# GpSimd's row scalings at fixed places, row tails in two parts, and one transpose for the softmax denominators of all eight heads

## The chip, the core and the metric

The kernel runs on one core of one Trainium2 chip. The metric is device time in microseconds (us) of one execution, less is better. Five engines matter: TensorE (PE in the profile, with its weight loads as PEld) multiplies matrices into PSUM, VectorE (DVE) and ScalarE (ACT) read PSUM and work element by element, GpSimd (POOL) works element by element on SBUF and issues transfers, and SyncE (SP) issues transfers. Each engine carries out its instructions in the order in which the program lists them; an instruction that waits holds back all that stand behind it on that engine.

## What is computed

One layer of a graph transformer with masked attention, two layer norms and a feed-forward part, and one more residual layer norm around the whole. F = 8 frames, N = 2048 rows, C = 256 channels, H = 8 heads of D = 32, all in float32:

```python
qkv = jnp.einsum('fnc,ck->fnk', x, w_qkv)                 # x: (8, 2048, 256)
q, k, v = jnp.split(qkv, 3, axis=-1)                      # each to (F, N, 8, 32)
scores = jnp.einsum('fnhd,fmhd->fhnm', q, k) / jnp.sqrt(D)
scores = jnp.where(adj > 0, scores, -1e9)                 # adj: (2048, 2048)
attn = softmax(scores, axis=-1)
t = jnp.einsum('fhnm,fmhd->fnhd', attn, v).reshape(F, N, C)
y = layernorm(x + t, ln1_g, ln1_b)
h = relu(einsum('fnc,cd->fnd', y, w1) + b1)
y = layernorm(y + einsum('fnd,dc->fnc', h, w2) + b2, ln2_g, ln2_b)
return layernorm(x + y)                                   # no gain, no offset
```

## The kernel before, in words

**Items.** The queries of a frame are cut into four chunks of 512 (`qc`), the heads into two groups of four (`g`), the keys into sixteen blocks of 128 (`mb`). An item is `(f, qc, g, mb)`; there are 8 x 4 x 2 x 16 = 1024, worked in that order. For one item TensorE makes the scores of 128 keys against 512 queries for four heads (`scores`, L230), VectorE adds the mask out of PSUM in two halves (L233), ScalarE takes the exponential in place (L237), and TensorE multiplies by V and accumulates over the 16 blocks (`values`, L249). The exponentials are never divided block by block; the sums over the keys (the denominators) are made apart.

**Denominators.** A group of 16 items leaves 16 tiles of exponentials in the pool `p` of 12 buffers. `add_up` adds most of them into three tiles: GpSimd adds blocks 3, 6, 8, 10, 12 and 14 into block 0 (L271), and transfers that accumulate, issued from GpSimd's queue (L268), add blocks 4, 7 and 11 into block 1 and 5, 9 and 13 into block 2. `denominator` then multiplies the three and block 15 by a matrix of ones (L315, 16 float32 matmuls in four blocks, each head's sum over 32 identical rows), ScalarE copies the result to `dT` (L317), TensorE turns `dT` in four transposes (L95, in `transposes`), and VectorE takes the reciprocal (L326) and notes the sum and the smallest sum (L327, L328). This is done for each half of the heads.

**Row tails.** When the second group of a chunk is done, `outcome` turns and divides the attention output (`divide`, L353), adds x by an accumulating transfer (L339), and starts `tail`: `norm`, `feed_forward` (two turns, two products by w1, the scaling of the rows by gain and offset on GpSimd at L459 and L461, two products by w2 whose results VectorE adds at L483), `norm`, a second scaling on GpSimd (L363, L365), x added by another accumulating transfer (L367), seven steps of waiting, `norm`, and the store (L370). A `norm` is four pairs of statistics on VectorE (L278, L279), four small GpSimd instructions (L283 to L287), and, two steps later, four scalings on ScalarE (L290). `y` has two buffers, so at most two tails are under way: a third `outcome` waits at `ROOM` until one has stored. The last chunk of all is finished by `finish`, in two half-tiles that take turns.

**Order of work.** The order on every engine is written out by the program, one step per item. Step t first calls `advance(t)`, which lets side work on; then it issues the exponential of item t + 1, the scores of item t + 2, and the values of item t. Side work is a list of generators, sorted by due step. `BANK` asks for the one PSUM bank of side work; one generator may take it in a step, and holds it while it answers `MORE` or `WAIT`. A holder that answers `MORE` goes on in the same step if at least 1024 of a credit are left (2200 come in with each step, and 512 columns in four heads cost 2048, a set of turns 1400) or if something that wants the bank is past its due step; otherwise it goes on in the next step. I call what fits one step at the usual rate a portion: one block of denominators, half of a projection, half of a w1 or w2 product pair, or one set of four turns. A number given to `yield` makes a generator sleep that many steps. Tails start ten steps after their `outcome` is due and are due 16 steps later still (the last but one: five and three). The work for the next frame (`turn`, `ask`, `project`) starts at the steps in `NEXT`; projected keys and values have 11 buffers each, of which a frame uses eight.

**After the items.** `while fill: advance(t, finish=True)` runs what is left, without credit. `finish` lists all steps of both halves in one go.

## Time and profile before

| what | value |
|---|---|
| median of 3 runs | 3196.82 us (3194.78 to 3200.07) |
| the profiled execution's own time | 3199.32 us |
| its span, first to last instruction | 3197.5 us |
| mean granted TensorE clock | 0.987 |
| busy: PE, DVE, POOL, ACT | 3098.8, 2737.4, 2589.4, 2438.4 us |
| turns of `dT`: 256 matmul instructions | 48.1 us busy |
| waits of TensorE for VectorE's mask additions, whole span | 35.6 us in 61 waits |
| the same between 200 and 3000 us | 11.0 us in 26 waits |

The profiled execution took 2.5 us more than the median, and 1.8 us of its time lie outside the span. Busy times are unions of an engine's instructions. Idle time of an engine that does not bound the kernel costs nothing, so the table has to be read with the question of which engine the others wait for. In a timeline row the first number is the start, the second the length over which merged instructions extend, and a bracket gives the idle time before and what ended it.

### The profile page before, as it was taken

To read this page: it belongs to the slowest core of one execution; us is meant where nothing else is said; L and a number is where in the kernel's file an instruction comes from. 1 tells how busy PE (TensorE), PEld (TensorE's weight loads), DVE (VectorE), ACT (ScalarE), POOL (GpSimd) and SP (SyncE) were. 2 spreads that over 40 slices of the span, in tenths; PEclk is the share of its full clock that TensorE was granted. 3 is DMA by queue.
4 is the path that set the end of the run, shared out by engine and by line. 5 is a ranking of instruction groups with operands and counts; after the bars stand their busy time and mean duration, and the time that the engine had idled before them with its cause. 6 is when DMAs were issued, how large, how long until landed. Compare 5 with 4: busy or idle time off the path is not lost.

```text
span 3197.5 us, 68542 instructions
## 1 busy us (share of the span) xinstructions
PE 3098.8 (97%) x28996; PEld 980.3 (31%) x28996; DVE 2737.4 (86%) x3203; ACT 2438.4 (76%) x1941; POOL 2589.4 (81%) x1358
## 2 busy tenths in 40 slices
PE   7899999999999999999999999999999999999985
PEld 4222333233332333323333323323233233332222
DVE  4788888888889988888988988888888888889975
ACT  3677778778778777788777788778878778778764
POOL 0478888888888888789888889888888788879884
PEclk8899999999999999999999999999999999999998
DMA  9588889788879888789878889878889788878863
GB/s 322 141 193 189 181 180 194 178 190 193 182 175 210 186 191 175 175 193 208 190 172 176 190 185 221 174 169 199 180 193 207 170 191 196 178 170 167 178 142 71
DMA packets 153098, 589.49 MB, mean 184 GB/s; under 512 B 15024, under 2 KB 67760, under 8 KB 103888
## 3 DMA queue, kind: packets, MB, share of 16 engines
q0 software_dynamic: 64272, 433.75, 67.7%
q1 hardware_dynamic: 87696, 149.98, 13.4%
q8 instruction: 229, 3.75, 0.4%
q10 hardware_dynamic: 816, 1.31, 0.1%
q14 instruction: 85, 0.70, 0.1%
HBM read 146.67 MB, written 37.75 MB: 58 GB/s over the span
## 4 chain that ended last, share of the span: by engine, by line
PE 87%; DVE 5%; issue 2%; DMA 1%; POOL 1%; ACT 1%; DVEq 0%; ACTq 0%; POOLq 0%
PE s L230 32%; PE x L249 28%; PE x L54 16%; PE x L315 7%; DVE p L233 4%; PE x L95 4%; DMA p<-p 1%; DVE st L278 0%; POOL p L271 0%; DMA y<-in_x_dram 0%; DVE y L353 0%; ACT p L237 0%; PE s L54 0%; DVE mv L279 0%; ACT y L290 0%
## 5 line engine op out<-in xcount | busy, mean ns | idle before, releaser
L233 DVE TENSOR_TENSOR p<-s,mask 128x1024 f32<-128x1024 f32 x2048 | 2410.3, 1219 | 336.2 <-PE s L230 196.0
L237 ACT ACTIVATE p<-p 128x2048 f32<-128x2048 f32 x1024 | 1956.6, 1911 | 527.7 <-DVE p L233 453.7
L271 POOL TENSOR_TENSOR p<-p 128x2048 f32<-128x2048 f32 x382 | 1858.7, 4866 | 388.5 <-ACT p L237 388.2
L230 PE MATMUL s<-qT,kT 32*128 32x512 f32 x8192 | 1172.4, 642 | 40.9 <-DVE p L233 35.6
L249 PE MATMUL x<-p,v 128*32 128x512 f32 x8192 | 1092.7, 605 | 0.5 <-ACT oT L253 0.4
L230 PEld LDWEIGHTS s<-qT,kT 32*128 32x128 f32 x8192 | 320.8, 183 | 643.9 <-DVE p L233 602.5
L268 POOL DMA_DIRECT2D p<-p x382 | 408.1, 1070 | 78.4 <-ACT p L237 49.4
L249 PEld LDWEIGHTS x<-p,v 128*32 128x32 f32 x8192 | 161.4, 108 | 779.9 <-issue 289.8
L315 PE MATMUL x<-p,ones 128*32 128x512 f32 x2080 | 267.1, 592 | 0.6 <-DMA p<-p 0.5
L54 PE MATMUL x<-in,wqkv 128*32 128x512 f32 x1888 | 243.5, 592 | 0.0
L290 ACT ACTIVATE y<-y,nb,rs 128x256 f32<-128x256 f32 x372 | 218.4, 590 | 3.0 <-POOL nb L287 3.0
L278 DVE BATCH_NORM_STATS2 st<-y 128x6 f32<-128x256 f32 x372 | 155.1, 417 | 5.2 <-DMA y<-in_x_dram 5.2
L54 PE MATMUL x<-turned,w1s 128*32 128x512 f32 x992 | 122.5, 592 | 0.0
L54 PEld LDWEIGHTS x<-wqkv,in 128*32 128x32 f32 x3584 | 102.2, 110 | 63.5 <-issue 58.9
L54 PE MATMUL x<-w2s,hT 128*32 128x256 f32 x2016 | 121.1, 381 | 0.0
L54 PE MATMUL x<-wqkv,in 128*32 128x128 f32 x3584 | 117.3, 273 | 0.0
L315 PEld LDWEIGHTS x<-p,ones 128*32 128x32 f32 x2080 | 67.4, 110 | 156.8 <-issue 152.0
L54 PEld LDWEIGHTS x<-in,wqkv 128*32 128x32 f32 x1888 | 61.7, 110 | 140.9 <-issue 113.1
L284 POOL TENSOR_TENSOR rs<-rs,mhalf 128x4 f32<-128x4 f32 x93 | 96.2, 1035 | 7.7
L363 POOL TENSOR_TENSOR y<-y,g2r 128x1024 f32<-128x1024 f32 x31 | 99.3, 3205 | 1.9 <-ACT y L290 1.9
L365 POOL TENSOR_TENSOR y<-y,be2r 128x1024 f32<-128x1024 f32 x31 | 91.9, 2963 | 0.6
L54 PEld LDWEIGHTS x<-w2s,hT 128*32 128x32 f32 x2016 | 65.5, 111 | 70.5 <-issue 37.8
(116 smaller groups left out, 1342.1 us busy)
## 6 DMA issues: line engine op xcount, KB each, us to landing
p<-p POOLq DMA_DIRECT2D x382, 1024.0 KB, 9.7
in<-xd SPq DMA_DIRECT2D x87, 512.0 KB, 9.3
mask<-md SPq DMA_DIRECT2D x248, 128.0 KB, 7.9
y<-in_x_dram POOLq DMA_DIRECT2D x62, 512.0 KB, 9.5
p<-in_adj_dram SPq DMA_DIRECT2D x16, 1024.0 KB, 9.7
out_dram<-y SPq DMA_DIRECT2D x31, 512.0 KB, 5.9
in<-in_x_dram SPq DMA_DIRECT2D x29, 512.0 KB, 14.5
xd<-in SPq DMA_DIRECT2D x28, 512.0 KB, 10.7
```

The costliest lines, as they stand in the source:

```text
L54: nc.tensor.matmul(out[r:r + D], lhsT[:, r:r + D], rhs, start=start, stop=stop)
L95: nc.tensor.transpose(ps[:, j * P:(j + 1) * P], s, ident)
L230: nc.tensor.matmul(ps2[half][:, j, :], KT[f, mb // TPC, g][r:r + D, (mb % TPC) * P:(mb % TPC + 1) * P], QT[f, qc, g][r:r + D, :], start=Tr ...
L233: nc.vector.tensor_tensor(pt[:, 2 * half:2 * half + 2, :], ps, MK[f, qc, mb // 2][:, mb % 2, None, :].to_broadcast([P, 2, CH]), ALU.add)
L237: nc.scalar.activation(PT[item], PT[item], AF.Exp, scale=1.0 / math.sqrt(D))
L249: nc.tensor.matmul(O[grp][r:r + D, :], V[f, mb // TPC, g][:, mb % TPC, r:r + D], PT[item][:, h, :], start=(mb == 0), stop=(mb == LAST))
L268: nc.gpsimd.dma_start(PT[f, qc, g, chain[0]], PT.pop(item), accum_op=ALU.add)
L271: nc.gpsimd.tensor_tensor(first, first, PT.pop(item), ALU.add)
L278: nc.vector.bn_stats(st, t[:, j, :])
L290: nc.scalar.activation(t[:, j, :], t[:, j, :], AF.Identity, bias=nb[:, j:j + 1], scale=rs[:, j:j + 1])
L315: nc.tensor.matmul(ps[r:r + D, :], cst["ones"], term[:, h, :], start=(n == 0), stop=(n == len(blocks) - 1))
L363: nc.gpsimd.tensor_tensor(z, z, rows(cst["g2r"]), ALU.mult)
```

## The change

It has four parts, in the words of the code.

1. **Denominators.** The ones are replaced by a matrix `halves` that has, for group g, ones in 16 of the 32 columns and zeros in the others. The sums of the two groups so land in different rows of a tile. For g = 0 ScalarE copies the PSUM tile to `dT` and the generator ends; for g = 1 VectorE adds the PSUM tile to it, `dT` is turned once for both, and one reciprocal and one pair of notes cover all eight heads. The fourth block of a group may come one step later.
2. **GpSimd's scalings.** Both instructions of a scaling are issued together, at a step chosen by `calm`: at once if the next block number is among 15, 0, 1, 2, 3, 4, otherwise not before block 15 comes. The first scaling runs in a generator of its own beside the w1 products, and the w2 products wait until four steps after it. `norm` leaves 2, 3 or 4 steps before its ScalarE part, by a table (`lag`).
3. **Tails in two parts.** What comes after the w1 products is a generator of its own (`closing`) with its own due step, 33 steps after the outcome's; the first part is due at 27. The last tail but one starts at 8 in place of 5, loads x into a tile and adds that on GpSimd (its offset `be2r` is not added in this branch) in place of the offset, the accumulating transfer and seven steps, and takes its last `norm` in one go. `finish` takes its tile from the pool `p` and sleeps a step between rounds from the fourth on.
4. **Buffers and places.** Keys and values have 10 buffers in place of 11, and five of the eight projections of a frame start later.

```diff
...
     dp = ctx.enter_context(tc.tile_pool(name="dp", bufs=1, space=bass.MemoryType.DRAM))
     mkp = ctx.enter_context(tc.tile_pool(name="mkp", bufs=MB // 2 + 1))
     ld = ctx.enter_context(tc.tile_pool(name="ld", bufs=LD))
-    kp = ctx.enter_context(tc.tile_pool(name="kp", bufs=3 * NCK - 1))
+    kp = ctx.enter_context(tc.tile_pool(name="kp", bufs=3 * NCK - 2))
     qp = ctx.enter_context(tc.tile_pool(name="qp", bufs=4))
-    vp = ctx.enter_context(tc.tile_pool(name="vp", bufs=3 * NCK - 1))
+    vp = ctx.enter_context(tc.tile_pool(name="vp", bufs=3 * NCK - 2))
     pp = ctx.enter_context(tc.tile_pool(name="pp", bufs=12))
     work = ctx.enter_context(tc.tile_pool(name="work", bufs=1))
     yp = ctx.enter_context(tc.tile_pool(name="yp", bufs=2))
...
         give(xT)
 
 
-    PT, O, OT, RC = {}, {}, {}, {}
+    PT, O, OT, RC, DT = {}, {}, {}, {}, {}
 
     def scores(item):
         f, qc, g, mb = item
...
             first = PT[f, qc, g, POOLED[0]]
             nc.gpsimd.tensor_tensor(first, first, PT.pop(item), ALU.add)
 
+
+    CALM = (LAST, 0, 1, 2, 3, 4)
+
+    def calm():
+        return 1 + (LAST - 1 - state["now"]) % MB if (state["now"] + 1) % MB not in CALM else 1
+
+    def lag():
+        return (4, 4, 4, 4, 2, 2, 2, 2, 2, 2, 3, 3, 3, 4, 4, 4)[state["now"] % MB]
 
     def norm(t, per=1):
         mv = small.tile([P, TPC, nc.vector.BN_AGGR_DIM], F32, name="mv")
...
         nb = small.tile([P, TPC], F32, name="nb")
         nc.gpsimd.tensor_tensor(nb, mv[:, :, 0], rs, ALU.mult)
         nc.gpsimd.tensor_scalar(nb, nb, -1.0, 1.0, op0=ALU.mult, op1=ALU.mult)
-        yield 2
+        yield lag()
         for j in range(TPC):
             nc.scalar.activation(t[:, j, :], t[:, j, :], AF.Identity, bias=nb[:, j:j + 1], scale=rs[:, j:j + 1])
             if j % per == per - 1:
...
     def denominator(f, qc, g, ready):
         grp = (f, qc, g)
         blocks = [ALONE, MOVED[0][0], POOLED[0], MOVED[1][0]]
-        late = {2: ready - 1, 3: ready}
+        late = {2: ready - 1, 3: ready + 1}
         if (f, qc, g) == items[-1][:3]:
             blocks = [POOLED[0], 11, 12, MOVED[0][0], 13, 14, MOVED[1][0], 15]
             late = {n: len(items) - k for n, k in ((2, 2), (3, 1), (4, 1), (5, 0), (6, 0), (7, 0))}
...
             state["credit"] -= 4 * CH
             for h in range(4):
                 r = D * h
-                nc.tensor.matmul(ps[r:r + D, :], cst["ones"], term[:, h, :], start=(n == 0), stop=(n == len(blocks) - 1))
-        dT = op.tile([P, CH], F32, name="dT")
-        nc.scalar.copy(dT, ps)
+                nc.tensor.matmul(ps[r:r + D, :], cst["halves"][:, g, :], term[:, h, :], start=(n == 0), stop=(n == len(blocks) - 1))
+        if g == 0:
+            DT[f, qc] = op.tile([P, CH], F32, name="dT")
+            nc.scalar.copy(DT[f, qc], ps)
+            return
+        dT = DT.pop((f, qc))
+        nc.vector.tensor_tensor(dT, ps, dT, ALU.add)
         yield 1
         yield BANK
         ps = bank()
         transposes(ps, [dT[:, j::TPC] for j in range(TPC)])
-        if g == 0:
-            RC[f, qc] = op.tile([P, TPC, H], F32, name="rc")
-        rc = RC[f, qc]
-        den = ps.rearrange("p (j c) -> p j c", c=P)[:, :, ::D]
-        nc.vector.reciprocal(rc[:, :, 4 * g:4 * g + 4], den)
+        rc = RC[f, qc] = op.tile([P, TPC, H], F32, name="rc")
+        den = ps.rearrange("p (j c) -> p j c", c=P)[:, :, ::D // 2]
+        nc.vector.reciprocal(rc, den)
         nc.vector.tensor_tensor(RS[:, 0], RS[:, 0], den, ALU.add)
         nc.vector.tensor_tensor(RS[:, 1], RS[:, 1], den, ALU.min)
-        if g == 1:
-            begin = items.index((f, qc, g, LAST)) + SUM + 2
-            start(begin, outcome(f, qc) if (f, qc) != (F - 1, NCK - 1) else finish(f, qc), begin)
+        begin = items.index((f, qc, g, LAST)) + SUM + 2
+        start(begin, outcome(f, qc) if (f, qc) != (F - 1, NCK - 1) else finish(f, qc), begin)
 
     def outcome(f, qc):
         yield ROOM
...
         nc.gpsimd.dma_start(y, xin, accum_op=ALU.add)
         begin = items.index((f, qc, 1, LAST)) + SUM + 2
         if (f, qc) == (F - 1, NCK - 2):
-            start(begin + 5, tail(f, qc, y, xin, 2), begin + 8)
+            xb = take([P, TPC, C], F32)
+            nc.sync.dma_start(xb, xin)
+            start(begin + 8, tail(f, qc, y, xin, begin + 11, 2, xb), begin + 11)
         else:
-            start(begin + 10, tail(f, qc, y, xin), begin + 26)
+            start(begin + 10, tail(f, qc, y, xin, begin + 33), begin + 27)
 
     def divide(f, qc, y):
         rc = RC.pop((f, qc))
...
             transposes(ps, [oT[:, j::TPC] for j in range(TPC)])
             nc.vector.tensor_tensor(y[:, :, gg * P:(gg + 1) * P].rearrange("p j (h d) -> p j h d", d=D),
                                     ps.rearrange("p (j h d) -> p j h d", h=4, d=D),
-                                    rc[:, :, 4 * gg:4 * gg + 4, None].to_broadcast([P, TPC, 4, D]), ALU.mult)
-
-    def tail(f, qc, y, xin, per=1):
+                                    rc[:, :, gg::2, None].to_broadcast([P, TPC, 4, D]), ALU.mult)
+
+    def tail(f, qc, y, xin, due, per=1, xb=None):
         yield from norm(y, per)
-        yield from feed_forward(y)
+        second = yield from feed_forward(y, xb is not None)
+        start(state["now"] + 1, closing(f, qc, y, second, xin, per, xb), due)
+
+    def closing(f, qc, y, second, xin, per, xb):
+        yield from second
         yield 1
         z = y
         yield from norm(z, per)
-        nc.gpsimd.tensor_tensor(z, z, rows(cst["g2r"]), ALU.mult)
-        yield 1
-        nc.gpsimd.tensor_tensor(z, z, rows(cst["be2r"]), ALU.add)
-        yield 1
-        nc.gpsimd.dma_start(z, xin, accum_op=ALU.add)
-        yield 7
-        yield from norm(z, per)
+        if xb is None:
+            yield calm()
+            nc.gpsimd.tensor_tensor(z, z, rows(cst["g2r"]), ALU.mult)
+            nc.gpsimd.tensor_tensor(z, z, rows(cst["be2r"]), ALU.add)
+            yield 1
+            nc.gpsimd.dma_start(z, xin, accum_op=ALU.add)
+            yield 7
+        else:
+            nc.gpsimd.tensor_tensor(z, z, rows(cst["g2r"]), ALU.mult)
+            nc.gpsimd.tensor_tensor(z, z, xb, ALU.add)
+            yield 2
+        yield from norm(z, per if xb is None else TPC)
         nc.sync.dma_start(out[f, qc * CH:(qc + 1) * CH, :].rearrange("(p j) c -> p j c", p=P), z)
         state["tails"] -= 1
 
...
         nc.sync.dma_start(dst[:, own], z)
 
     def finish(f, qc):
-        y = yp.tile([P, TPC, C], F32, name="y")
+        y = pp.tile([P, 4, CH], F32, name="p")[:, 0:2, :].rearrange("p a (b c) -> p (a b) c", c=C)
         xr, xb = state["rows"]
         yield from divide(f, qc, y)
         yT, hT = (work.tile([P, 2, CH], F32, name=n) for n in ("turned", "hT"))
         dst = out[f, qc * CH:(qc + 1) * CH, :].rearrange("(p j) c -> p j c", p=P)
         both = [half_rows(h, y, xr, xb, yT, hT, dst) for h in range(2)]
+        rounds = 0
         while both:
             for e in list(both):
                 if next(e, both) is both:
                     both.remove(e)
-
-    def feed_forward(y):
+            rounds += 1
+            if rounds > 3:
+                yield 1
+
+    def feed_forward(y, soon):
         yield TURNED
         state["turned"] = True
         yT = work.tile([P, 2, CH], F32, name="turned")
...
             ps = bank()
             transposes(ps, [y[:, j, a * P:(a + 1) * P] for j in range(TPC)])
             nc.scalar.activation(yT[:, a, :], ps, AF.Identity, bias=cst["be1c"][:, a:a + 1], scale=cst["g1c"][:, a:a + 1])
-        yield 1
-        nc.gpsimd.tensor_tensor(y, y, rows(cst["g1r"]), ALU.mult)
-        yield 1
-        nc.gpsimd.tensor_tensor(y, y, rows(cst["be1b2r"]), ALU.add)
+        scaled = []
+
+        def scale():
+            nc.gpsimd.tensor_tensor(y, y, rows(cst["g1r"]), ALU.mult)
+            nc.gpsimd.tensor_tensor(y, y, rows(cst["be1b2r"]), ALU.add)
+            scaled.append(state["now"])
+
+        def later():
+            yield calm()
+            scale()
+
+        if soon:
+            scale()
+        else:
+            start(state["now"], later(), state["now"])
         hT = work.tile([P, 2, CH], F32, name="hT")
         for d in range(2):
             yield BANK
...
                 columns(ps, w1s[:, a, d * P:(d + 1) * P], yT[:, a, :], start=(a == 0), stop=(a == 1))
             nc.scalar.activation(hT[:, d, :], ps, AF.Relu, bias=cst["b1s"][:, d:d + 1], scale=1.0)
         state["turned"] = False
-        yield 1
+        return second_products(y, hT, scaled)
+
+    def second_products(y, hT, scaled):
+        while not scaled or state["now"] < scaled[0] + 4:
+            yield 1
         z = y
         for jj in range(0, TPC, 2):
             yield BANK
...
         give(xT)
 
     NEXT = {1: [(turn, 0)], 2: [(ask, 1)], 20: [(turn, 1)], 34: [(ask, 2)], 40: [(project, 0, 0)], 50: [(turn, 2)],
-            60: [(project, 1, 0)], 66: [(ask, 3)], 72: [(turn, 3)], 80: [(project, 2, 0)], 98: [(ask, 0)], 100: [(project, 3, 0)],
-            104: [(project, 0, 1)], 108: [(project, 1, 1)], 112: [(project, 2, 1)], 116: [(project, 3, 1)]}
+            60: [(project, 1, 0)], 66: [(ask, 3)], 72: [(turn, 3)], 98: [(ask, 0)], 100: [(project, 2, 0)],
+            104: [(project, 3, 0)], 108: [(project, 0, 1)], 112: [(project, 1, 1)], 116: [(project, 2, 1)], 120: [(project, 3, 1)]}
 
     def begin():
         todo = deque((qc, c) for qc in range(NCK) for c in range(NCK))
...
     nc.gpsimd.memset(cst["ones"], 1.0)
     cst["mhalf"] = const.tile([P, TPC], F32, name="mhalf")
     nc.gpsimd.memset(cst["mhalf"], -0.5)
-    RS = const.tile([P, 2, TPC, H // 2], F32, name="RS")
+    cst["halves"] = const.tile([P, 2, D], F32, name="halves")
+    nc.gpsimd.memset(cst["halves"], 0.0)
+    for g in range(2):
+        nc.gpsimd.memset(cst["halves"][:, g, g * D // 2:(g + 1) * D // 2], 1.0)
+    RS = const.tile([P, 2, TPC, H], F32, name="RS")
     nc.gpsimd.memset(RS[:, 0], 0.0)
     nc.gpsimd.memset(RS[:, 1], 1.0)
```

## The prediction

> **What bounds the kernel now.** I read three views first: the page's head, the windows, and the waits between 200 and 3000 us.
>
> ```profile
> PE 3098.8 (97%) x28996; PEld 980.3 (31%) x28996; DVE 2737.4 (86%) x3203; ACT 2438.4 (76%) x1941; POOL 2589.4 (81%) x1358
> ```
>
> ```profile
> 1500.00:2000.00 500.00, 498.59 (x4692) 156.18 (x4692) 438.46 (x506) 395.72 (x316) 426.86 (x220) 1.00 0.85 190
> 3000.00:3100.00 100.00, 88.56 (x708) 24.50 (x708) 86.44 (x106) 73.73 (x57) 88.23 (x50) 0.95 0.79 165
> ```
>
> ```profile
> PE s L230 <- DVE p L233: 11.0, 26, 0.7
> ```
>
> The window's columns are length, busy PE, PEld, DVE, ACT and POOL, then granted clock. From about 100 to 2900 us TensorE is busy without a break, at full clock, and waits 11.0 us in all; the others have 12% or more to spare. GpSimd, which half of the diff is about, is waited for almost nowhere: the addition at L271 kept TensorE's loads waiting 1.3 us in the whole run. So the middle is bought with TensorE time alone, and VectorE (86%) is next.
>
> How much an instruction of TensorE is worth is seen in its timeline, cut at the first score matmul of each item (L230):
>
> ```profile
> 3058.06 1.04 PE L315 MATMUL x<-p,ones 128*32 128x512 f32 x8
> 3059.03 1.14 PE L230 MATMUL s<-qT,kT 32*128 32x512 f32 x8
> ...
> 3061.95 1.14 PE L230 MATMUL s<-qT,kT 32*128 32x512 f32 x8
> 3063.02 1.06 PE L249 MATMUL x<-p,v 128*32 128x512 f32 x8
> 3064.02 0.75 PE L95 MATMUL x<-ident,dT 128*128 128x128 f32 x4
> 3064.70 1.14 PE L230 MATMUL s<-qT,kT 32*128 32x512 f32 x8
> ...
> 3094.00 1.14 PE L230 MATMUL s<-qT,kT 32*128 32x512 f32 x8 [0.42 <-DVE p L233]
> 3095.07 1.07 PE L249 MATMUL x<-p,v 128*32 128x512 f32 x8
> 3096.55 1.14 PE L230 MATMUL s<-qT,kT 32*128 32x512 f32 x8 [0.41 <-DVE p L233]
> ```
>
> The step with one block of denominators lasts 2.92 us (3059.03 to 3061.95), the one that turns `dT` 2.75, an empty one 2.55, because two mask additions keep VectorE 2 x 1.22 us. I cut all steps of items 33 to 895 so (863 steps, 2572.3 us): 109 hold two portions (3.78 to 3.81 us), 16 are empty, the rest hold one. One more portion in a step costs 0.86 us, so scores and values alone cost TensorE 2.92 - 0.86 = 2.06.
>
> At the end two things stand out, in the timelines of VectorE, TensorE and the stores:
>
> ```profile
> 3081.76 0.43 DVE L278 BATCH_NORM_STATS2 st<-y 128x6 f32<-128x256 f32 x1 [5.23 <-DMA y<-in_x_dram]
> 3084.20 2.09 PE L230 MATMUL s<-qT,kT 32*128 32x512 f32 x8 [6.61 <-DVE p L233]
> ```
>
> ```profile
> 3184.66 3.94 SPq L435 DMA_DIRECT2D out_dram<-y  x2
> 3193.33 0.33 SPq L370 DMA_DIRECT2D out_dram<-y  x1
> ```
>
> The last tail but one starts its statistics before x has been added to its rows; VectorE stands 5.23 us, and TensorE behind it. And the store that ends the kernel is not that of the last chunk (second of L435, about 3188.3) but that of this same tail, whose last statistics the program lists behind all of `finish`.
>
> **The change, part by part.** The sum is against the profiled execution, 3199.3 us.
>
> *Denominators.* Of 64 sets of four turns 32 go. A set takes TensorE 0.68 us (3064.02 to 3064.70). Frames 0 to 6 have 28 chunks: 28 x 0.68 = 19.0 us, if the step is filled with other work or a double step becomes a single one; if the step stays empty it gets shorter by 2.75 - 2.55 = 0.20 only. I take 19.0, because the list of side work is longer than the steps: a chunk has 36 portions for 32 steps (35 after), which is why 109 steps were double. The 16 matmuls of a group keep their shapes. ScalarE loses 32 copies of 0.585 us (L317), 18.7; it is not waited for, worth nothing. VectorE gains 32 additions as at L483, 0.69 each, 22 us, and loses 32 sets of L326 to L328 (240 + 111 + 158 ns, 16 us); 6 us more in 2737, hidden by its 12% in the middle. Behind the addition stand the next mask additions: at 3061.98 the denominators ended and the copy began at 3062.09, a mask addition at about 3062.6, so 0.69 us of addition holds it back 0.2 us, less than the 0.3 us that VectorE idles in such a step. The side bank comes free 0.1 us later than by the copy; its next user starts 2 us later. The fourth block's extra step changes nothing: at one block a step, from step 2, it never came before step 5.
>
> *Empty steps.* Each costs 2.55 - 2.06 = 0.49 us of TensorE. The w2 products were past due in every middle chunk (52 banks, each both portions in one step); with the later due step about half should spread. Moving projections from step 80 to 100 and on thins out the third quarter of a frame (27 portions for its 32 steps). Bounds: all 16 vanish, -7.8 us; two more per frame, +7. The two moves oppose each other; I take 0.
>
> *GpSimd's scalings, `lag`.* Nearly the same instructions at other steps; the nearest rows of what they could free are waits of 1.3 us (TensorE's loads for L271) and 3.0 us (ScalarE L290 for L287). I take 0. What they make longer is the tail, see the second rival. The buffers and the three GpSimd fills at the start (0.17 us each, as L812, after the identity is made) cost nothing: TensorE waits there for x and the identity.
>
> *Last frame.* It has 27 empty steps of 127, for lack of the next frame's work. Four sets of turns at 0.20 are 0.8; a few double steps that spread into empty ones (0.49 each) another 1.2: -2, bounds -0.8 and -4.7.
>
> *The stall at 3076.* The tail starts three steps later, some 3 x 2.45 us for VectorE, more than the 5.23 it stood. But its `outcome` waits for the first tail of the frame, which is longer now: counted in steps below it stores one step later than `outcome` ran before, and then x's transfer stands behind one more addition of 4.9 us on GpSimd's queue. So 7.4 - 4.9 = 2.5 us of the 5.23 go. TensorE lost 6.61 for 5.23; I take -3. Bounds -6.3 (step of 8.75 us to an empty one of 2.49) and 0.
>
> *The end.* If the last norm of this tail is listed ahead, the end is the store at 3188.3: -5.0. Against it: its second norm now reaches ScalarE only behind the last exponentials and `oT` (3151.6). 2.1 us of scalings (L290 x4) and two GpSimd instructions of 2.4 end at about 3158.6. Its four statistics stand on VectorE between the two divisions of `finish`, which went at 3155.6 and 3156.2, and take 2.1 us: the second division moves to 3160.8, +4.6. I take 0, bounds -5.0 and +4.6.
>
> Sum: -19.0 - 2 - 3 = -24.0, that is 3175.3. The profiled execution took 2.5 more than the median: 3173.
>
> *A rule that speaks against it.* TensorE's steps got longer by 0.86 us per portion in the rows above. The Trainium skill, "Perfetto Trace Analysis", Identifying the Most-Contended Engine, says that matmul busy time is no good measure of TensorE's headroom and to judge by the weight loads' share, here 31%. By that TensorE has room and the 19.0 would be 0: 3192. The rows decide for me, since 109 double steps show what a portion costs.
>
> **Rivals.**
>
> *All of it counts.* Empty steps vanish, the stall goes whole, the end is the earlier store: 19.0 + 7.8 + 4.7 + 6.3 + 5.0 = 42.8, so 3154. For it: later due steps spread the doubles. Against it: the longer tail and the thinner third quarter.
>
> *The tail gets too long (slower).* From the step in which `outcome` is due: statistics at 10 to 13, ScalarE at 18, turns at 22, first scaling at 26, the next group's denominators hold the bank from 28 to 31, w2 at 32 to 34, second norm from 35, ScalarE at 42, second scaling at 47, transfer at 48, third norm from 55, ScalarE at 63, store at 67. Before, it was 58. The third `outcome` is due at 64 and so waits three steps, and its own tail starts at 74 whether x has come or not. In the trace the latest of these transfers was issued at 1361.23, landed 9.3 us later (the median) and was used at 1374.43, 3.9 us to spare. One step later it stands behind an addition of 5.1 us and comes 1.2 us late, 3.6 with the longest landing (11.7). VectorE then stands, in all 28 chunks, with all mask additions behind it: at 2 us, 56 us, 3173 + 56 = 3229. It decides from 24/28 = 0.86 us per chunk. A second norm that begins one step later than 35 misses its place, and `calm` sends the scaling ten steps on: worse. Against it: step 67 leaves the transfer where it was in the latest case.
>
> *Freed steps stay empty.* VectorE becomes the bound in them: 32 x 0.20 + 3 = 9.4, so 3187. For it: 2.55 against 2.75 in the rows; against it: 36 portions for 32 steps.
>
> *It does not do what it says:* the turns are covered by VectorE anyway, the end is eaten by the additions: 3197.
>
> **How the numbers follow.** Likeliest, 3163 to 3183: 0.58. All of it, below: 0.14. Empty steps, 3183 to 3194: 0.16, a quarter of it within 0.2%, which is about what can be told here (6.4 us: 3190.4 to 3203.2). Tail too long: 0.10, four fifths of it slower. Nothing: 0.02. Faster 0.58 + 0.14 + 0.12 = 0.84; same 0.04 + 0.02 + 0.02 = 0.08; slower 0.08. The range runs from the rival of all gains, 3153, into that of empty steps, 3191.
>
> **What would show it.** 128 turns of `dT` in place of 256, about 24 us busy; PE busy near 3077; additions of 0.69 us at the new line; fewer w2 steps with both portions. The 5.23 us wait halved. The middle step count: if empty steps rise over 30, the third rival. If VectorE's statistics wait for `y<-in_x_dram` in the middle, the second. I am wrong if the tails' order makes VectorE or GpSimd late in every chunk, which this trace cannot show.

## The result: 8.4% slower, and the profile after

| | before | changed |
|---|---|---|
| median | 3197.40 us (3194.78 to 3200.07, 4 runs) | 3464.62 us (3457.25 to 3471.02, 4 runs) |
| ratio | | 1.0835, 95% interval 1.0811 to 1.0859 |
| span of the profiled execution | 3197.5 us | 3460.7 us |
| mean granted clock of TensorE | 0.987 | 0.957 |
| start, to item 33 | 181.8 us | 180.6 us |
| items 33 to 896 | 2572.3 us | 2807.0 us |
| the last frame's items | 388.5 us | 417.1 us |
| the end, after the last item | 55.0 us | 56.0 us |

The forecast was 3173 us. The loss is in the middle, where I had expected the gain: 234.7 of the 263.1 us lie between items 33 and 896, 8.7 us in each of 27 chunks. The head of the page and the window that the prediction showed (length, busy PE, PEld, DVE, ACT and POOL, granted clock, DMA share, GB/s) now read:

```profile
PE 3174.1 (92%) x28868; PEld 979.4 (28%) x28868; DVE 2750.9 (79%) x3139; ACT 2422.2 (70%) x1909; POOL 2595.0 (75%) x1360
```

```profile
1500.00:2000.00 500.00, 466.18 (x4188) 142.05 (x4188) 399.95 (x455) 353.58 (x277) 387.32 (x199) 0.95 0.79 174
```

TensorE idles 34 us in 500, where before it idled 1.4. No engine has taken its place: VectorE has fallen from 86% to 79%. So something makes all of them stand together. The waits of the changed kernel between 200 and 3200 us (who waits for whom: total, times, longest) say what:

```profile
POOL p L268 <- DMA p<-p: 114.1, 43, 4.6
...
PE s L230 <- DVE p L233: 99.5, 90, 4.6
DVE p L233 <- DMA p<-p: 96.0, 33, 7.4
DVE y L364 <- DMA out_dram<-y: 63.5, 17, 5.2
PE x L95 <- DVE y L364: 58.1, 17, 4.9
...
PE x L323 <- DMA p<-p: 31.1, 16, 4.4
```

Two transfers hold VectorE: a store (`out_dram<-y`, 63.5 us) and the accumulating transfers of exponentials (`p<-p`, 96.0 us). The second also holds TensorE itself, when it comes to multiply the sums for the denominators (L323, 31.1 us). None of these waits was among the rows of before. In the timeline the first is seen between 2174 and 2190 us:

```profile
2174.00 0.34 SPq L390 DMA_DIRECT2D out_dram<-y  x1
...
2185.43 0.69 DVE L364 TENSOR_TENSOR y<-x,rc 128x512 f32<-128x512 f32 x1 [4.11 <-DMA out_dram<-y]
2186.18 0.75 PE L95 MATMUL x<-ident,oT 128*128 128x128 f32 x4 [3.80 <-DVE y L364]
2187.85 2.09 PE L230 MATMUL s<-qT,kT 32*128 32x512 f32 x8 [0.92 <-DVE p L233]
```

The division of a new chunk writes into the buffer of `y` from which an older tail is being stored. The program lets it go as soon as the store is *listed*; on the chip it must wait until the store has *landed*, 11.3 us later. Mask additions stand behind it on VectorE, scores behind those. The second follows 40 us later here, with GpSimd's queue:

```profile
2221.35 2.38 POOL L380 TENSOR_TENSOR y<-y,g2r 128x1024 f32<-128x1024 f32 x1
2223.80 2.39 POOL L381 TENSOR_TENSOR y<-y,be2r 128x1024 f32<-128x1024 f32 x1
2226.12 0.90 POOL L268 DMA_DIRECT2D p<-p  x1
...
2227.32 1.50 POOL L268 DMA_DIRECT2D p<-p  x1
...
2235.98 2.35 DVE L233 TENSOR_TENSOR p<-s,mask 128x1024 f32<-128x1024 f32 x2 [6.98 <-DMA p<-p]
...
2237.26 2.09 PE L230 MATMUL s<-qT,kT 32*128 32x512 f32 x8 [4.25 <-DVE p L233]
```

The second scaling (two instructions, 4.8 us together) stands ahead of the transfers that add blocks 4 and 5 away. Those are issued some 5 us late, the buffers of `p` come free late, and VectorE has no place for the next mask addition. It stands so twice: 6.98 us until the first of the two transfers has landed, and 5.06 us more, to 2243.40, until the second has. The places differ from chunk to chunk: these 12 us come once in a frame, some 3 us in the chunk after, and TensorE's own wait at the denominators, 1.0 to 4.4 us, in the two after that. The chain of waits, in order of time (start, length, what), has a row for the store and one for the second of the two transfers:

```profile
2174.00 11.31 DMA out_dram<-y
...
2227.32 15.95 DMA p<-p
```

### The profile page after: what moved, and what is told of

The parts are those of the page before. It is cut to its first block, busy times and chain, and to the rows that moved or that the text cites. A ratio compares the mean times of both kernels' runs of the same rounds, so it can differ in the third digit from the quotient of the medians.

```text
span 3460.7 us, 68235 instructions
## 1 busy us (share of the span) xinstructions
PE 3174.1 (92%) x28868; PEld 979.4 (28%) x28868; DVE 2750.9 (79%) x3139; ACT 2422.2 (70%) x1909; POOL 2595.0 (75%) x1360
## 3 DMA queue, kind: packets, MB, share of 16 engines
q0 software_dynamic: 64128, 433.22, 62.7%
## 4 chain that ended last, share of the span: by engine, by line
PE 37%; DMA 29%; DVE 15%; POOL 9%; ACT 4%; issue 3%; POOLq 0%; DVEq 0%; ACTq 0%
DMA p<-p 23%; PE s L230 15%; DVE p L233 12%; PE x L249 11%; PE x L54 7%; DMA out_dram<-y 6%; POOL p L271 4%; PE x L323 3%; ACT p L237 2%; POOL y L381 2%; POOL y L380 2%; DVE st L286 1%; POOL rs L292 1%; PE x L95 1%; DVE y L364 1%
## 5 line engine op out<-in xcount | busy, mean ns | idle before, releaser
L230 PE MATMUL s<-qT,kT 32*128 32x512 f32 x8192 | 1206.2, 659 | 130.5 <-DVE p L233 123.5
L249 PE MATMUL x<-p,v 128*32 128x512 f32 x8192 | 1122.2, 621 | 0.0
L268 POOL DMA_DIRECT2D p<-p x382 | 372.1, 989 | 255.7 <-DMA p<-p 122.4
L230 PEld LDWEIGHTS s<-qT,kT 32*128 32x128 f32 x8192 | 329.1, 188 | 774.5 <-DVE p L233 710.8
L323 PE MATMUL x<-p,halves 128*32 128x512 f32 x2080 | 272.4, 602 | 32.6 <-DMA p<-p 32.6
L291 POOL TENSOR_SCALAR rs<-mv 128x4 f32<-128x4 f32 x93 | 17.9, 193 | 189.9 <-DVE mv L287 184.9
L323 PEld LDWEIGHTS x<-p,halves 128*32 128x32 f32 x2080 | 66.5, 111 | 196.8 <-issue 135.7
L348 POOL DMA_DIRECT2D y<-in_x_dram x31 | 26.8, 865 | 118.8 <-DVE y L364 114.2
L95 PE MATMUL x<-ident,oT 128*128 128x128 f32 x252 | 50.3, 326 | 65.6 <-DVE y L364 65.6
## 6 DMA issues: line engine op xcount, KB each, us to landing
p<-p POOLq DMA_DIRECT2D x382, 1024.0 KB, 10.3
p<-in_adj_dram SPq DMA_DIRECT2D x16, 1024.0 KB, 10.3
out_dram<-y SPq DMA_DIRECT2D x31, 512.0 KB, 10.7
```

The source lines that it names most:

```text
L95: nc.tensor.transpose(ps[:, j * P:(j + 1) * P], s, ident)
L230: nc.tensor.matmul(ps2[half][:, j, :], KT[f, mb // TPC, g][r:r + D, (mb % TPC) * P:(mb % TPC + 1) * P], QT[f, qc, g][r:r + D, :], start=Tr ...
L249: nc.tensor.matmul(O[grp][r:r + D, :], V[f, mb // TPC, g][:, mb % TPC, r:r + D], PT[item][:, h, :], start=(mb == 0), stop=(mb == LAST))
L268: nc.gpsimd.dma_start(PT[f, qc, g, chain[0]], PT.pop(item), accum_op=ALU.add)
L323: nc.tensor.matmul(ps[r:r + D, :], cst["halves"][:, g, :], term[:, h, :], start=(n == 0), stop=(n == len(blocks) - 1))
```

## The experiments

The questions: do these two waits carry the loss; which part of the change brings each; and is the denominators' gain real? Below, "middle" is the length of items 33 to 896 in the profiled execution; times are medians, ratios are against the kernel before on the same chip.

### e1: the denominators alone

The kernel before, with part 1 of the change, but without the extra step for the fourth block, and nothing else.

```diff
...
-                nc.tensor.matmul(ps[r:r + D, :], cst["ones"], term[:, h, :], start=(n == 0), stop=(n == len(blocks) - 1))
-        dT = op.tile([P, CH], F32, name="dT")
-        nc.scalar.copy(dT, ps)
+                nc.tensor.matmul(ps[r:r + D, :], cst["halves"][:, g, :], term[:, h, :], start=(n == 0), stop=(n == len(blocks) - 1))
+        if g == 0:
+            DT[f, qc] = op.tile([P, CH], F32, name="dT")
+            nc.scalar.copy(DT[f, qc], ps)
+            return
+        dT = DT.pop((f, qc))
+        nc.vector.tensor_tensor(dT, ps, dT, ALU.add)
...
```

> The kernel before, with the denominators of both halves summed in one tile and turned once, and nothing else of the change. Theory A (a set of turns costs TensorE 0.68 us, and the loss of the whole change lies in the longer tail alone): 13 to 22 us faster, ratio 0.993 to 0.996, and no wait of the division for a store. Rival R (the addition on VectorE or the later turn delays the order and so causes part of the loss): slower than before, ratio above 1.002.

3194.13 us, ratio 0.9995 (0.9986 to 1.0005): no difference, where I had expected 13 to 22 us. Cut into steps, the middle shows why:

| steps of items 33 to 895 | before | e1 |
|---|---|---|
| empty | 16 of 2.55 us | 17 of 2.55 |
| turns of `dT` | 54 of 2.75 | 27 of 2.98 |
| other turns | 160 of 2.72 | 160 of 2.77 |
| one portion | 524 of 2.93 | 574 of 2.93 |
| two portions | 109 of 3.79 | 85 of 3.79 |

The freed steps did fill up: 24 double steps became single, and no step stayed empty. Some 16 us were won (27 x 2.75 and 24 x 3.79 gone, 50 x 2.93 and one of 2.55 come). They were paid back at two places. The 27 steps that still turn `dT` are 0.23 us longer, 6 us in all. And in the second frame a turn of `in` was due before its rows had come, twice, which with what follows cost most of the rest:

```profile
609.79 0.66 PE L95 MATMUL x<-ident,in 128*128 128x128 f32 x4 [4.06 <-DMA in<-in_x_dram]
```

### e2 and e5: a third buffer for `y`, and a third tail

e2 is the changed kernel with one more buffer, so that the division no longer meets the store; e5 also lets three tails be under way.

```diff
-    yp = ctx.enter_context(tc.tile_pool(name="yp", bufs=2))
+    yp = ctx.enter_context(tc.tile_pool(name="yp", bufs=3))
...
-                elif e[2] == TURNED and state["turned"] or e[2] == ROOM and state["tails"] == 2:
+                elif e[2] == TURNED and state["turned"] or e[2] == ROOM and state["tails"] == 3:
```

(The second pair of lines is e5's alone.)

> The changed kernel with three buffers for the rows y in place of two; the order on every engine stays the same. Theory A (the first division of a chunk waits for the store of the tail two chunks before, because it writes into that tail's buffer; 71.5 us of VectorE waits in the trace): that wait is gone and with it its followers, 100 us or more come back, about 3330 to 3370 us. Theory B (GpSimd's second scaling and the transfer of x stand ahead of the accumulating transfers of blocks 4 and 5, whose sums then come late for the buffers of p; 99.3 us of VectorE waits): only some 70 us come back, waits of VectorE's mask additions for p stay near 100 us, and the time stays above 3370 us.

> The changed kernel with three buffers for y and three tails allowed at once, so that a division waits neither for a place nor for a store. If what is left of the loss after the third buffer (3371 us) lay in the divisions coming late (step 4 after they are due), it goes: below 3250 us. If it lies in theory B (the second scaling, two GpSimd instructions of 2.4 us, and the transfer of x ahead of the accumulating transfers of blocks 4 and 5): VectorE's waits for p stay near 110 us, and the time stays between 3320 and 3370 us.

e2: 3370.74 us, 1.0541 (1.0524 to 1.0559), middle 2735.7: 71.3 us less than the changed kernel. e5: 3371.49 us, 1.0549 (1.0533 to 1.0565), middle 2723.7; between e2 and e5 the medians can't tell a difference. In e2 the wait for the store is gone from the list, and the other has stayed (columns as above):

```profile
DVE p L233 <- DMA p<-p: 110.6, 35, 7.2
```

So the store was worth 71 of the 235 us, a little more than the 63.5 us that its row showed for the time from 200 to 3200 us. The Trainium skill, "Perfetto Trace Analysis", Optimization Strategy, reads a gap that repeats on the engine which should be full as a possible lack of memory for the next tile, the number of buffers among it. That fits the first gap. The second comes back as well, in every frame, and a buffer more of `y` left it where it was: it is another tile's.

### e4: the store late, in the kernel before

The counter-test: the kernel before, whose third norm now waits six steps longer, so that its store is listed six steps later; in the changed kernel it is nine.

```diff
         nc.gpsimd.dma_start(z, xin, accum_op=ALU.add)
-        yield 7
+        yield 13
         yield from norm(z, per)
```

> The kernel before with 13 in place of 7 steps of sleep ahead of the last norm of a tail: nothing but the store is later, by 6 steps (step 62 to 64 after the division was due, where the changed kernel has 67). Theory A: the division of the chunk after next now waits for the store, 1 to 5 us in most chunks, 40 to 150 us slower. Theory B alone: same as before within 10 us.

3280.82 us, 1.0260 (1.0243 to 1.0278), middle 2652.7, 80 us over before. The same wait appears, with nothing else of the change in it:

```profile
DVE y L353 <- DMA out_dram<-y: 61.4, 12, 8.1
PE x L95 <- DVE y L353: 59.3, 14, 7.6
```

Late by itself, the store costs about what the changed kernel loses by it (80 us here, 71 there).

### e3 and e6: the places of GpSimd's scalings

e3 is the changed kernel without fixed places: `calm` always answers 1, `lag` always 2, as before the change. e6 is e5 with two blocks fewer on the list of places, so that the second scaling, which had landed just ahead of block 4's transfer (46 steps after the outcome was due), is put off to step 57. The transfer of x, the third norm and the store move with it.

```diff
-        return 1 + (LAST - 1 - state["now"]) % MB if (state["now"] + 1) % MB not in CALM else 1
+        return 1
...
-        return (4, 4, 4, 4, 2, 2, 2, 2, 2, 2, 3, 3, 3, 4, 4, 4)[state["now"] % MB]
+        return 2
```

```diff
-    CALM = (LAST, 0, 1, 2, 3, 4)
+    CALM = (LAST, 0, 1, 2)
```

> The changed kernel with the fixed places undone: calm answers 1 and lag answers 2 always, the rest of the change as it is. If the loss comes from the length of the tail or from where the second scaling stands (A or B): the tail is some 8 steps shorter, the waits for the store and for p go, and the time is 3165 to 3200 us. If it comes from the tail in two parts, the due steps, the 10 buffers or the moved projections (rival C): it stays above 3350 us.

> As the run with three tails, but calm does not count blocks 3 and 4 among its places any more; the second scaling so goes from step 46 to step 58, where block 15 comes, and the transfer of x ahead of block 1. Theory B: VectorE's waits for p fall below 30 us and the time to 3180 to 3230 us. If B is wrong: within 20 us of the run with three tails.

e3: 3297.24 us, 1.0316 (1.0299 to 1.0333), middle 2661. With two buffers of `y` both waits are nearly gone (`p<-p` 10.7 us), since the tail is short again. Yet it is not the kernel before: a new wait has come, here in its timeline:

```profile
1457.64 4.79 POOL L271 TENSOR_TENSOR p<-p 128x2048 f32<-128x2048 f32 x1
...
1464.43 0.60 ACT L298 ACTIVATE y<-y,nb,rs 128x256 f32<-128x256 f32 x1 [9.07 <-POOL nb L295]
...
1466.88 1.93 PE L249 MATMUL x<-p,v 128*32 128x512 f32 x8 [7.24 <-ACT p L237]
```

A norm's four small GpSimd instructions stand behind the two instructions of a scaling and two additions (the last of them is the first row here), and two steps later ScalarE has to have their result. Seven such places cost TensorE 55.9 us. In five frames, besides, four portions of projections come into one step with a set of the division's turns, and that step takes 9.6 to 11.2 us; no run shows what brings them together. Parts 2 and 3 thus hang together, as far as e3 shows: without the table of places, the other order of the tail loses here instead. My expectation that undoing the places would bring the time back missed.

e6: 3265.11 us, 1.0213 (1.0197 to 1.0228), middle 2635.2: 88.5 us less than e5 for eleven steps' delay of two instructions per chunk. VectorE's wait, of 109.9 us in e5, reads

```profile
DVE p L233 <- DMA p<-p: 11.1, 6, 2.6
```

and TensorE's row for L323 is gone. That settles the second wait. The time is still 35 us above the 3230 that I had expected at most. What is left, 63 us over before, is hardly a wait for a transfer any more. It sits in steps 4 to 6 after the outcome is due (3.42, 4.08 and 3.86 us, before 2.83, 2.88 and 2.85), and there e6's window and timeline show a full VectorE:

```profile
1570.00:1580.00 10.00, 8.21 (x64) 2.37 (x56) 9.80 (x23) 5.61 (x3) 5.34 (x3) 1.00 0.99 198
```

```profile
1574.07 0.41 DVE L286 BATCH_NORM_STATS2 st<-y 128x6 f32<-128x256 f32 x1
1574.52 0.18 DVE L287 BATCH_NORM_AGGREGATE mv<-st 128x2 f32<-128x6 f32 x1
1574.62 0.67 DVE L364 TENSOR_TENSOR y<-x,rc 128x512 f32<-128x512 f32 x1
1575.21 0.42 DVE L286 BATCH_NORM_STATS2 st<-y 128x6 f32<-128x256 f32 x1
1575.66 0.18 DVE L287 BATCH_NORM_AGGREGATE mv<-st 128x2 f32<-128x6 f32 x1
1575.76 2.34 DVE L233 TENSOR_TENSOR p<-s,mask 128x1024 f32<-128x1024 f32 x2
```

One step holds a division and statistics of two norms, of two different tails, besides its mask additions.

### e9 and e12: the statistics moved out of each other's way

e9 is e6 with both later norms moved by some steps; e12 moves the second norm five steps more.

```diff
         yield from second
-        yield 1
+        yield 6
...
-            yield 7
+            yield 11
```

(e12: `yield 11` in place of `yield 6`.)

> The kernel of the run before (e6: changed kernel, three y buffers, three tails, second scaling ahead of block 3) with two waits longer: `yield 6` in place of `yield 1` ahead of the second norm, and `yield 11` in place of `yield 7` ahead of the third. The second scaling stays at step 58. What moves is when VectorE computes the statistics: the second norm's go from steps 35-38 after the division is due to 40-43, the third norm's from 66-69 to 70-73, so that neither falls on the steps 3-6 of the next chunk, in which the reciprocal and the two divisions of the next outcome run. Theory (VectorE is full in those steps, 9.80 of 10 us in one window of e6, and what remains of e6's loss of 63 us in items 33-896 is that stack): steps 4-6 fall from 3.43, 4.11 and 3.86 us to about 2.9 each, 27 chunks of 2.6 us or 60 to 70 us less in all, and the time is 3180 to 3215 us. Rival (the remaining loss is the longer tail itself: store, buffers and p's transfers, whichever steps the statistics have): within 15 us of e6's 3265, with the long steps at other places.

> The kernel e9 with the wait ahead of the second norm five steps longer again (`yield 11` in place of `yield 6`). In e9 the statistics of the second and the third norm fell on the same steps, 9-13 after the division is due, two a step, and steps 9-12 took 3.12, 3.24, 3.30 and 3.34 us in place of 2.93, though one statistics of 0.6 us fits into the 0.58 us that VectorE idles in a step of 2.93 us. Theory (the price is in the stack, not in the place): with the second norm's on steps 14-18 and the third's alone on 9-13, steps 9-12 are back to 2.93 to 2.97 us, 27 chunks of 1.2 us or some 32 us less in items 33-896, and the time is 3195 to 3205 us. Rival (VectorE's work of the tails is too much wherever it lies, or the second scaling moves again): within 10 us of e9's 3230, with steps 14-18 longer by what steps 9-12 gain.

e9: 3230.45 us, 1.0109 (1.0094 to 1.0125), middle 2597.0. e12: 3211.26 us, 1.0046 (1.0030 to 1.0061), middle 2580.2. Mean length of the steps concerned over the 27 chunks, in us, cut as before:

| step | before | e6 | e9 | e12 |
|---|---|---|---|---|
| 4 | 2.83 | 3.42 | 2.75 | 2.75 |
| 5 | 2.88 | 4.08 | 2.89 | 2.88 |
| 6 | 2.85 | 3.86 | 2.84 | 2.84 |
| 9 | 2.93 | 2.93 | 3.13 | 2.93 |
| 10 | 2.93 | 2.93 | 3.25 | 2.93 |
| 11 | 2.77 | 2.93 | 3.30 | 2.93 |
| 12 | 2.93 | 2.93 | 3.34 | 2.93 |
| 14 | 2.94 | 2.97 | 2.92 | 2.99 |
| 21 | 2.88 | 3.04 | 3.05 | 3.29 |

e9 emptied steps 4 to 6 and gained 38 us in place of my 60 to 70, because the two norms' statistics now fell together on steps 9 to 13. e12 took them apart, and those steps are as before; it gained 17 us in the middle in place of 32, since steps 20 to 24 grew. Part of that is the second wait, which comes back: VectorE waits for `p` 16.8 us between 200 and 3200 us, up to 3.8 us at a time, where in e6 it was 11.1 and 2.6. In steps 9 to 12, then, one set of statistics costs nothing, and two cost 0.2 to 0.4 us; VectorE's mask additions leave some 0.58 us of a step of 2.93, and one set takes 0.60.

The loss in the middle is thus taken apart, each kernel changed from the one before it:

| | middle, us | step, us |
|---|---|---|
| changed kernel | 2807.0 | |
| third buffer of `y` (e2): the store's wait | 2735.7 | -71.3 |
| third tail (e5) | 2723.7 | -12.0 |
| second scaling elsewhere (e6): `p`'s transfers | 2635.2 | -88.5 |
| statistics off the divisions (e9) | 2597.0 | -38.2 |
| statistics apart (e12) | 2580.2 | -16.8 |
| left against the kernel before | 2572.3 | -7.9 |

Each length is that of one profiled execution, and runs of one of these kernels lie 4 to 14 us apart, so the third tail's 12 us, which the medians do not show, may be nothing. The medians of the whole kernel, last frame and end included, fall by 93.9, rise by 0.8, and fall by 106.4, 34.7 and 19.2 us at the five changes. The shares hold for this order; in another the overlap of the waits would fall to other lines. Of the last frame's 28.6 us all are gone in e12 (386.8 us for 388.5 before). What stays open is its end, 62.7 us in place of 55.0, and why the middle is not below that of before.

### e7: buffers and places of the projections

The kernel before with part 4 alone.

```diff
-    kp = ctx.enter_context(tc.tile_pool(name="kp", bufs=3 * NCK - 1))
+    kp = ctx.enter_context(tc.tile_pool(name="kp", bufs=3 * NCK - 2))
...
-            60: [(project, 1, 0)], 66: [(ask, 3)], 72: [(turn, 3)], 80: [(project, 2, 0)], 98: [(ask, 0)], 100: [(project, 3, 0)],
+            60: [(project, 1, 0)], 66: [(ask, 3)], 72: [(turn, 3)], 98: [(ask, 0)], 100: [(project, 2, 0)],
...
```

> The kernel before with 10 buffers for keys and values and the projections at the changed steps, nothing else. Theories A and B: nothing, within 10 us of before. Rival C (these two moves thin out the third quarter of a frame or make it wait): 15 us slower or more.

3197.68 us, 0.9999 (0.9989 to 1.0008). It costs and brings nothing.

### e8, e10 and e11: the parts that pay

e8 is the kernel before with the shared denominators, `turn` two steps later (against the wait seen in e1), and, for the last tail but one only, x and its offset added by GpSimd in place of the accumulating transfer, that tail started two steps later, and its last norm listed in one go. e10 starts that tail at 5 again and gives its first norm four steps for the roots; e11 keeps e8's start and takes only the four steps.

```diff
         yield INPUTS - 2
...
-        yield 5
+        yield 7
         yield from turn_rows(xc, xT)
...
-            start(begin + 5, tail(f, qc, y, xin, 2), begin + 8)
+            xb = take([P, TPC, C], F32)
+            nc.sync.dma_start(xb, xin)
+            start(begin + 7, tail(f, qc, y, xin, 2, xb), begin + 10)
...
-        yield from norm(y, per)
+        yield from norm(y, per, 2 if xb is None else 4)
...
+            nc.gpsimd.tensor_tensor(z, z, xb, ALU.add)
+            yield 2
+        yield from norm(z, per if xb is None else TPC)
```

(The line with `else 4` is in e10 and e11 only.)

> The kernel before with the shared denominators, with two more steps between the load of a chunk of x for the next frame and its turn (in the first run TensorE waited 7.9 us for such loads), and with the last tail but one begun two steps later, x added to it on GpSimd and its last norm ahead of the last chunk's work. By the step lengths the denominators give 17, the loads 8, the stall of the last tail but one 3 to 6, the end 2 to 4: 3165 to 3178 us. If the freed TensorE time is taken up elsewhere: within 6 us of before.

> The kernel e8 (before with shared denominators, a later turn, a last-but-one tail with x and its bias added by GpSimd) with that tail begun two steps sooner and its first norm's scalings put two steps later (4 in place of 2 after the roots). In e8 ScalarE waited 3.35 us there for GpSimd's four small instructions, which stood behind an addition of 5.5 us, one of 3.33 us and two transfers, and one step took 7.1 us. With the roots listed ahead of that addition the wait goes: 3 to 4 us less than e8, 3179 to 3181 us. Rival: the four small instructions still end behind some addition, or VectorE's statistics come into a full step: within 1 us of e8's 3183.5.

> The kernel e8 with the last-but-one tail begun where e8 begins it and only its first norm's scalings two steps later (4 in place of 2 after the roots). In e10, where the tail was also begun two steps sooner, ScalarE's wait for the roots was gone, but VectorE's statistics waited 4.80 us for x's transfer into y instead, and the time was 1.1 us over e8's. Theory (a tail there has both waits, and each start that avoids one meets the other unless the scalings are given more steps): without either wait, 3 us less than e8, 3179 to 3182 us. Rival: the two steps that the scalings are later are paid at the end, where the tail's store is the last but one to land: within 1 us of e8's 3183.5.

| | median, us | ratio to before | middle | last frame | end |
|---|---|---|---|---|---|
| e8 | 3183.48 | 0.9954 (0.9940 to 0.9967) | 2562.0 | 382.2 | 55.3 |
| e10 | 3184.62 | 0.9961 (0.9948 to 0.9975) | 2562.1 | 384.8 | 55.9 |
| e11 | 3179.52 | 0.9948 (0.9934 to 0.9961) | 2562.1 | 378.9 | 57.3 |

All three are faster than both kernels, by 0.4 to 0.5% against the one before; for e8 that is less than the 3165 to 3178 us that I had expected. In the middle the shared denominators are worth 10.3 us, once the loads come in time. (The later `turn` was not run alone; in the kernel before, TensorE does not wait for these loads between 200 and 3000 us.) The 6 us that the `dT` steps still lose are seen in e8's timeline:

```profile
1528.19 1.14 PE L230 MATMUL s<-qT,kT 32*128 32x512 f32 x8
...
1528.81 0.68 DVE L321 TENSOR_TENSOR dT<-x,dT 128x512 f32<-128x512 f32 x1
...
1529.40 0.42 DVE L278 BATCH_NORM_STATS2 st<-y 128x6 f32<-128x256 f32 x1
1529.86 0.18 DVE L279 BATCH_NORM_AGGREGATE mv<-st 128x2 f32<-128x6 f32 x1
1529.95 2.33 DVE L233 TENSOR_TENSOR p<-s,mask 128x1024 f32<-128x1024 f32 x2
...
1531.22 1.14 PE L230 MATMUL s<-qT,kT 32*128 32x512 f32 x8 [0.21 <-DVE p L233]
```

The new addition falls on a step that already has statistics: 0.68 + 0.60 us, and the step takes 3.03 us. e10 shows a trade: in e8 ScalarE waited 3.35 us for the roots; with the tail two steps sooner that wait is gone, and VectorE waits for x instead:

```profile
3067.52 0.43 DVE L278 BATCH_NORM_STATS2 st<-y 128x6 f32<-128x256 f32 x1 [4.80 <-DMA y<-in_x_dram]
```

e11 has neither of the two waits, though one for the roots of the tail before has grown from 1.00 us (e8) to 3.38: its last frame is 3.3 us shorter than e8's, and its end 2.0 us longer, as its rival had it. Its median is the lowest of all, but the intervals of e8 and e11 overlap, so that which of the two is faster stays open.

## Why the prediction was wrong

*GpSimd's scalings, `lag`: "I take 0".* This is the step that failed. My reason was that hardly anybody waited for GpSimd in the rows of before (1.3 and 3.0 us), and that the instructions are nearly the same. The same paragraph went on that what they make longer is the tail; I had the steps of the longer tail right (second scaling at 46 to 47, store at 67), but I priced the instructions by what they free, not by what stands behind them at the new place. Behind the second scaling stood two transfers of `p`, which I never followed: 88.5 us in place of 0. Two sets of statistics, moved with the tail, met each other and the division: 38.2 and 16.8 us.

*"The tail gets too long (slower)"* had the right sign, at a chance of 0.10, but the wrong wait. I had the third `outcome` wait at `ROOM`, and x's transfer come late for the statistics. The changed kernel's statistics waited for x 3.5 us in the whole run, one time. `ROOM` opens when the store is listed; the buffer is free when it has landed. Between the two stood the division, for 71 us. I counted steps of the written order and left out the landing of the transfer, although the page of before gives it: 5.9 us for `out_dram<-y`, two steps. With the store listed at 67 and the division of the chunk after next at 68, that alone made it late; in the changed kernel the store took 10.7 us.

*Denominators: 19.0.* Right in kind, and mis-sized: 10.3 us in e8, and nothing in e1, where the two late loads ate the rest. Of the loss of 0.23 us in each `dT` step I had written that the addition of 0.69 us would hold the mask additions back 0.2 us, "less than the 0.3 us that VectorE idles in such a step". I had read that at 3062 us, and the statistics of that step stand beside it in the trace (3062.56, 0.42 us); in e8's timeline the sum with them no longer fits. Against the third rival, the freed steps were filled (16 empty steps before, 17 in e1).

*Empty steps: 0.* Held for part 4 (the middle of e7 is 2573.6 us, before 2572.3) and for the denominators.

*Last frame: -2, and the stall at 3076: -3.* The last frame became 28.6 us longer by the same mechanisms as the middle; e12 has it 1.7 us shorter than before. The wait for x went from 5.2 us to 3.5. With the loads and roots in place (e11) it could have been 9.6 us shorter.

*The end: 0.* It became 1.0 us longer, within the bounds of -5.0 and +4.6.

*The rule that I weighed* spoke of the weight loads' share alone. The Trainium skill, "Perfetto Trace Analysis", Identifying the Most-Contended Engine, names beside it the share of the peak rate that the matmuls reach (MFU), which I did not work out. e1's 2.3 us, median against median, are nearer to the rule's 0 than to my 19.0, but not for its reason: the steps show some 16 us won and paid back elsewhere. The share fell from 31% to 28% while the kernel became slower; the steps' lengths stayed the better guide, and they were right on what a portion costs.

"I am wrong if the tails' order makes VectorE or GpSimd late in every chunk, which this trace cannot show" is what came, if not in every chunk alike. But it could be shown in part: the division's step, the store's landing and the queue behind step 46 all stand in the trace of before.

## What to carry to other kernels

When an order is written out in steps, a buffer is free when the transfer out of it has landed, not when it is listed: add the landing from the page to every count of steps that ends in a reuse. When an instruction moves on an engine that nobody waits for, list what is queued behind it at its new place, transfers first, and ask which buffer each of them frees. And on an engine with 0.6 us to spare in a step, what counts is not its share over the run, but whether two things of 0.6 us come into one step.

## What the runs showed of the hardware

I had not expected a stall to be paid twice. After the long ones, TensorE itself is slow. In the timelines above, eight score matmuls take 2.09 us after the stall, where they take 1.14 otherwise. Windows of 20 us (columns as above; the granted clock is the first number after the five engines):

```profile
2160.00:2180.00 20.00, 20.00 (x196) 6.69 (x192) 17.79 (x21) 13.75 (x11) 16.37 (x10) 1.00 0.50 106
2180.00:2200.00 20.00, 15.15 (x157) 5.36 (x156) 13.41 (x18) 9.24 (x8) 16.14 (x11) 0.91 1.03 210
...
2220.00:2240.00 20.00, 15.75 (x148) 4.50 (x144) 9.62 (x9) 11.28 (x9) 16.95 (x9) 0.88 0.69 147
```

With full work the clock is 1.00, in the windows with a stall 0.91 and 0.88. Over the run, the changed kernel's 28868 matmul instructions keep TensorE busy 3174.1 us, e1's as many 3081.0: 93 us of the 267 by which its span is longer than e1's are busy time, at a lower clock. In the profile's record of the clock the changed kernel has 36 stretches at 0.50 between 200 and 3200 us, each 3.4 or 6.8 us long, 205 us in all. A stretch begins near each of the 17 places where TensorE idled 3.4 us or longer, at the latest 5.2 us after the idle time began. Of the 21 idle times of 2.0 to 3.4 us, 18 have one, of the 15 of 1 to 2 us, two. The Trainium skill, "TensorE: Matmul & The Clock Gate", Part 1: The HAM clock gate, gives a reason: TensorE's clock is halved after a window of some 3.4 us without work, and full again after about as long a stretch of work. The lengths of the stretches agree with that. The idle time does not have to be so long: in e12 2.31 us were enough (at 2073.24, with no other stall near), and the measurement decides. In the first timeline TensorE idles 3.80 us; the four turns right behind it still take 0.75 us, as elsewhere, at a granted clock of 1.00. From 2187.6 to 2191.0 the clock is 0.50, and the score matmuls take 1.8 times as long (2.09 us for 1.14). At 2192.25, with the clock at 1.00, they take 1.14 again.
